# A convolution pair: the results' stores on GpSimd's queue, and the square of the Laplacian in the place of the smoothed sums

## The chip, the cores and the metric

The kernel runs on one core of one Trainium2 chip. The metric is device time in microseconds. The kernel before took 4897.4 us, the median of three runs (4884.03 to 4911.76 us).

The engines are TensorE (PE in the profile, its weight loads PEld), VectorE (DVE), ScalarE (ACT), GpSimd (POOL) and SyncE (SP), which here only issues transfers. Each takes its instructions in a fixed order.

## The reference

The input `x` has 4 images of 512 channels, 64 by 64 pixels, float32. Two layers follow each other.

Layer 0 is a linear attention: three 512 by 512 projections to queries, keys and values; a 5 by 5 depthwise and a grouped 1 by 1 convolution of these; an attention over 128 heads of 8 channels; a projection with batch normalisation; and `x` added. Call its result y. Layer 1, cut to what matters:

```python
sobel_h = dwconv(x, K_SX)
sobel_v = dwconv(x, K_SY)
sobel = jnp.sqrt(sobel_h ** 2 + sobel_v ** 2 + 1e-08)
lap = jnp.abs(dwconv(x, K_LAP))
diag = jnp.maximum(jnp.abs(dwconv(x, K_D1)), jnp.abs(dwconv(x, K_D2)))
grad = jnp.sqrt(sobel ** 2 + lap ** 2 + 1e-08)
E = jnp.stack([sobel, lap, diag, grad])
y = jnp.einsum('kbchw,koc->kbohw', E, w_branch) + b_branch[:, None, :, None, None]
# batch normalisation and Gelu; a gate per channel from the image's mean
z = jnp.einsum('bchw,oc->bohw', ef, w_fuse) + b_fuse[None, :, None, None]
mu = z.mean(axis=1, keepdims=True)
var = ((z - mu) ** 2).mean(axis=1, keepdims=True)
zn = (z - mu) / jnp.sqrt(var + LN_EPS)
out = jax.nn.gelu(zn * ln_gamma[None, :, None, None] + ln_beta[None, :, None, None], approximate=False)
return out + x
```

## The kernel before, in words

Channels lie on the 128 partitions, four chunks of 128 to an image. Layer 0 goes image by image in four groups of heads (`Group`): projections (L268, L290), the convolution as small matmuls (L402), correlations (L457), divisions; GpSimd issues the copies of the projected strips (L283), SP the loads of `x` and of `near` (L442).

Layer 1 of an image has three stages, each a Python generator. `project_out` makes y and writes it to DRAM. `edge_branches` reads windows of y and makes the four edge maps (`edges`), which TensorE takes to the branches (L738); `store` writes them out. `fuse_out` loads them (L892), multiplies by the fusion weights (`fuse`, L850), normalises, adds y and stores the result (`norm`).

For images 0 to 2 these stages are spread by shares of time (`advance`, SHARE_ and WAIT_ constants) between the steps of the next image's layer 0. For the last image nothing follows: its edge maps are made in windows of 8 rows instead of 4 and interleaved with its own projection and then with the third image's fusion, and its own fusion ends the kernel. TensorE's order is that of the program (`manual_schedule`). The order on the other engines comes from a scheduler that works from the dependences between tiles, so an edit of one tile can reorder them.

`edges` works on a window of two chunks. `dv` (one buffer) holds `down` and `smooth`, the differences and the sums of rows (L707 to L709). `maps` (three buffers) takes the diagonal and one Sobel term (L714), the Laplacian `lap` (L716 to L718) and the other Sobel term (L728, L729). ScalarE squares the Laplacian into `lap2` (L720), takes absolute values (L724) and squares the Sobel terms (L730). VectorE adds these (L731) and makes `grad` from `lap2` and the sum (L733), and ScalarE takes the roots (L734). With one `dv`, the next window's L707 has to wait for the last use of this one's.

`fuse` evicts each product twice, as a square (L852) and as `z` (L855 or L857, eight or six `z` buffers). `norm` takes the variance matmul (L866), its root (L868) and reciprocal (L869), multiplies (L877), takes Gelu (L878), and adds y from `yr`, which has two buffers (L874, L881). Then SP stores `z` (L882). A piece is 512 pixels of all four chunks; the very last 512 are two pieces of 256. There are 132 stores in all. One image's `fuse` of a piece is followed by the `norm` of the piece before.

All pools of layer 1 are stacks in SBUF, so a tile that is gone moves those behind it. TensorE's results go to PSUM, where the tag `ps` has four banks.

Of the kernel before, what the change touches and what calls it, by code (L numbers as in the profile page):

```python
# [8 lines left out]
F32 = mybir.dt.float32  # L9
# [6 lines left out]
P = 128  # L16
# [73 lines left out]
def conv_seq_kernel(  # L90
    ctx: ExitStack, tc, x, wqkv, dpk, wtab, proj, projc, pwk, bn0, consts, vec, watt1, batt1, watt2, wbr, wfuse, out
):
    nc = tc.nc
# [18 lines left out]
    def ps_tile(name):  # L112
        return psum.tile([P, 512], F32, tag="ps", name=name)
# [8 lines left out]
    def rows(ap, width=W):  # L122
        return ap.rearrange("p (r c) -> p r c", c=width)
# [99 lines left out]
    first = ExitStack()  # L223
# [449 lines left out]
    def edge_branches(b, efs, pool_sb, side):  # L673

        y = ys[b % 2]
        with ExitStack() as stack:
            pool = stack.enter_context(tc.tile_pool(name=f"E{b}", bufs=2, side=side, reuse_waits="tile"))
# [8 lines left out]
            run = WB * tall - 2  # L686
            yield 0.0

            def edges(u, pair):

                win = pool.tile([P, 2, (tall + 2) * WB], F32, name="win", tag="win")
                nc.sync.dma_start(
                    out=win,
                    in_=y[2 * pair : 2 * pair + 2].rearrange("c p r w -> p c (r w)")[
                        :, :, tall * u * WB : (tall * u + tall + 2) * WB
                    ],
                )
                above, mid, below = (win[:, :, n * WB : (n + tall) * WB] for n in range(3))
                maps = pool.tile([P, 4, 2, tall * WB], F32, name="maps", tag="maps", bufs=3)
                flat = maps.rearrange("p k c x -> p (k c x)")  # L700
                lap, sobel, grad = (maps[:, n, :, 0:run] for n in (0, 2, 3))


                dv = pool.tile([P, 2, 2, tall * WB], F32, name="dv", tag="dv", bufs=1)
                down, smooth = dv[:, 0], dv[:, 1]
                dvs = dv.rearrange("p k c x -> p (k c x)")
                nc.vector.tensor_sub(down, below, above)  # L707
                nc.vector.tensor_add(smooth, below, above)
                nc.vector.scalar_tensor_tensor(smooth, mid, 2.0, smooth, ALU.mult, ALU.add)  # L709

                half = 2 * tall * WB
                nc.vector.tensor_sub(flat[:, half : 3 * half - 2], dvs[:, 2 : 2 * half], dvs[:, 0 : 2 * half - 2])  # L714

                nc.vector.tensor_add(lap, mid[:, :, 0:run], mid[:, :, 2 : run + 2])  # L716
                nc.vector.scalar_tensor_tensor(lap, mid[:, :, 1 : run + 1], -6.0, lap, ALU.mult, ALU.add)
                nc.vector.tensor_add(lap, lap, smooth[:, :, 1 : run + 1])  # L718
                lap2 = pool.tile([P, 2, run], F32, name="lap2", tag="lap2", bufs=1)
                nc.scalar.activation(lap2, lap, AF.Square)  # L720
                first, second = (
                    maps[:, n : n + 2].rearrange("p k c x -> p (k c) x")[:, :, 0:run] for n in (0, 2)
                )
                nc.scalar.activation(first, first, AF.Abs)  # L724


                sv = flat[:, 3 * half : 4 * half - 2]
                nc.vector.tensor_add(sv, dvs[:, 0 : half - 2], dvs[:, 2:half])  # L728
                nc.vector.scalar_tensor_tensor(sv, dvs[:, 1 : half - 1], 2.0, sv, ALU.mult, ALU.add)  # L729
                nc.scalar.activation(second, second, AF.Square)  # L730
                nc.vector.tensor_add(sobel, sobel, grad)  # L731

                nc.vector.scalar_tensor_tensor(grad, lap2, SOBEL_EPS, sobel, ALU.add, ALU.add)  # L733
                nc.scalar.activation(second, second, AF.Sqrt, bias=sobel_eps)  # L734
                return maps
# [25 lines left out]
            if side == "left":  # L761

                banks = None
                for n in range(2 * steps + 1):
                    made = edges(n // 2, n % 2) if n < 2 * steps else None
                    yield 1.0
                    if n:
                        u, pair = divmod(n - 1, 2)
                        if pair == 0:
                            banks = quad_tiles("br")  # L770
                        for k in (1, 2, 0, 3):
                            for c in (2 * pair, 2 * pair + 1):
                                product(banks[k], k, c, held)
                        if pair:
                            for ks in ((1, 2), (0, 3)):
                                store(u, ks, [banks[k] for k in ks])
                    held = made
                yield 0.0
                return

            held = []
            for u in range(steps + 1):
                first = [edges(u, 0)] if u < steps else []
                yield share if u else share + WAIT_E
                if held:
                    branches(u - 1, (1, 2), held)
                    yield share
                    branches(u - 1, (0, 3), held)
                    yield share
                if first:  # L790
                    held = first + [edges(u, 1)]
                    yield share if u else share + WAIT_E

    def fuse_out(b, efs, pool_sb, side):

        y = ys[b % 2]
        with ExitStack() as stack:
            pool = stack.enter_context(tc.tile_pool(name=f"F{b}", bufs=2, side=side, reuse_waits="tile"))
# [63 lines left out]
            def norm(piece, zs, total):  # L862
                j, first, end = piece
                n, high = end - first, (end - first) // W
                ps = ps_tile("var")[:, :n]
                nc.tensor.matmul(ps, lhsT=ones, rhs=total, start=True, stop=True)  # L866
                rstd = pool.tile([P, 512], F32, name="rstd", tag="rstd", bufs=1)[:, :n]
                nc.scalar.activation(rstd, ps, AF.Sqrt, bias=ln_eps, scale=1.0 / C)  # L868
                nc.vector.reciprocal(rstd, rstd)  # L869
                at = 8 * j + first // W + 1  # L870
                for c in range(NCH):
                    z = zs[c]
                    yr = pool.tile([P, 8 * WB], F32, name="yr", tag="yr")[:, : high * WB]
                    nc.sync.dma_start(  # L874
                        out=yr, in_=y[c].rearrange("p r w -> p (r w)")[:, at * WB : (at + high) * WB]
                    )
                    nc.vector.tensor_mul(z, z, rstd)  # L877
                    nc.scalar.activation(  # L878
                        z, z, AF.Gelu, bias=vec_sb[:, V_LNB, c : c + 1], scale=vec_sb[:, V_LNG, c : c + 1]
                    )  # L880
                    nc.gpsimd.tensor_add(rows(z), rows(z), rows(yr, WB)[:, :, 1 : W + 1])  # L881
                    nc.sync.dma_start(out=out[b, c, :, 512 * j + first : 512 * j + end], in_=z)  # L882

            held = None
            for piece in pieces + [None]:
                if piece:
                    j, first, end = piece
                    n = end - first
                    ef = []
                    for k in range(4):  # L890
                        t = pool.tile([P, 512], F32, name="ef", tag="ef", bufs=8)[:, :n]
                        nc.sync.dma_start(out=t, in_=efs[j][:, k, first:end])  # L892
                        ef.append(t)
                    zs = []
                    total = pool.tile([P, 512], F32, name="total", tag="total")[:, :n]
                    fuse(0, ef, zs, total, n)
                    yield share
                    fuse(1, ef, zs, total, n)
                    yield share
                else:  # L900
                    yield 6.0
                if piece and late:
                    fuse(2, ef, zs, total, n)
                    yield share
                if held:
                    norm(*held)
                    yield share
                if piece:
                    for c in range(3 if late else 2, NCH):
                        fuse(c, ef, zs, total, n)  # L910
                        yield share
                    held = piece, zs, total
# [210 lines left out]
```

## Time and profile before

| what | value |
|---|---|
| median of three runs | 4897.4 us |
| the profiled execution, its own time | 4899.17 us |
| its span, first to last instruction | 4897.4 us |
| busy, TensorE / VectorE / ScalarE / GpSimd | 4649.1 / 2100.3 / 1592.8 / 1112.1 us |
| results' stores on SP (L882) | 132, 337 to 433 ns each to issue |
| strips' and maps' stores on GpSimd (L283, L751) | 1024 and 112, median 533 and 744 ns each to issue |
| L733, once a window | 112, of them 16 in the last image |

A line of a group gives the line of the kernel, engine, operation, the tile written and those read, the count and the durations. A line of waits gives who waited for whom, the total in us, how often, and the longest. A line of a timeline gives start and length in us, then engine, line and operation. A wait is put down to the engine whose event came last, and idle time of an engine that isn't on the path costs nothing.

### The profile page before, as it was taken

How to read it: one execution, taken by the hardware profiler on the slowest of the kernel's cores; microseconds unless marked ns; L12 is line 12 of the kernel's file. 1: busy time of each engine (PE TensorE's matmuls, PEld its weight loads, DVE VectorE, ACT ScalarE, POOL GpSimd, SP SyncE). 2: the span in 40 equal slices, each digit the busy share in tenths (PEclk: the TensorE clock that was granted, in tenths of full speed). 3: DMA queues.
4: the chain of work that ended last, by engine and by line, in shares of the span. 5: the costliest groups of instructions: out<-in, count | busy, mean ns of one | idle time of the engine just before them, and what ended most of it. 6: DMA issues, size and time to landing. Idle time of an engine off the chain costs nothing. (4 is left out here: it accounts for less than half of the span.)

```text
span 4897.4 us, 107513 instructions
## 1 busy us (share of the span) xinstructions
PE 4649.1 (95%) x46140; PEld 2691.9 (55%) x46140; DVE 2100.3 (43%) x2788; ACT 1592.8 (33%) x2723; POOL 1112.1 (23%) x1535
## 2 busy tenths in 40 slices
PE   9999999999999999899899999999999999899987
PEld 5666655455666565454466666455446565444433
DVE  1222222114655625311356553441125656437966
ACT  2111111002544524300245453430014545214765
POOL 3222212111221214311122121441112211011443
PEclk9999999999999999999999999999999999999998
DMA  6444456565656666676466666567556555554445
GB/s 204 136 126 136 141 182 199 163 165 157 206 174 202 188 207 187 214 188 171 142 200 195 190 195 203 175 210 211 153 172 186 183 174 176 164 160 148 158 146 171
DMA packets 469228, 864.12 MB, mean 176 GB/s; under 512 B 193000, under 2 KB 225800, under 8 KB 450320
## 3 DMA queue, kind: packets, MB, share of 16 engines
q1 hardware_dynamic: 415760, 721.90, 48.8%
q0 software_dynamic: 52992, 135.35, 9.0%
q8 instruction: 363, 5.95, 0.5%
q14 instruction: 113, 0.93, 0.1%
HBM read 575.93 MB, written 213.98 MB: 161 GB/s over the span
## 5 line engine op out<-in xcount | busy, mean ns | idle before, releaser
L268 PE MATMUL proj<-xt,w_sb 128*128 128x512 f32 x2048 | 937.6, 601 | 17.3 <-ACT rq L279 6.9
L661 PE MATMUL yps<-hd,fold_sb 128*128 128x512 f32 x2048 | 905.4, 599 | 18.4 <-DMA hd<-heads 14.9
L283 POOL DMA_DIRECT2D inp<-strip x1024 | 546.4, 536 | 1285.2 <-ACT strip L274 1253.5
L402 PE MATMUL cv<-inp,mat 32*32 32x512 f32 (+1 forms) x20480 | 734.5, 597 | 62.8 <-issue 50.2
L661 PEld LDWEIGHTS yps<-hd,fold_sb 128*128 128x128 f32 x2048 | 386.7, 191 | 508.1 <-issue 464.3
L268 PEld LDWEIGHTS proj<-xt,w_sb 128*128 128x128 f32 x2048 | 377.0, 191 | 475.2 <-issue 447.4
L402 PEld LDWEIGHTS cv<-inp,mat 32*32 32x32 f32 x20480 | 439.6, 103 | 325.7 <-issue 172.1
L850 PE MATMUL zps<-ef,wf_sb 128*128 128x512 f32 (+1 forms) x1056 | 467.2, 595 | 29.2 <-ACT z L855 17.2
L290 PEld LDWEIGHTS val<-w_sb,xt 128*128 128x128 f32 x4096 | 469.8, 192 | 34.4 <-issue 20.2
L290 PE MATMUL val<-w_sb,xt 128*128 128x128 f32 x4096 | 484.4, 277 | 0.5 <-DVE z L857 0.5
L274 ACT COPY strip<-proj 128x512 f32<-128x512 f32 x256 | 149.0, 582 | 989.9 <-PE proj L268 950.8
L738 PE MATMUL br<-maps,wbr_sb 128*128 128x256 f32 (+1 forms) x1792 | 468.3, 414 | 0.3 <-ACT ef_o L746 0.3
L666 DVE SCALAR_TENSOR_TENSOR yt<-yps,shift,xr 128x512 f32<-128x512 f32 x128 | 95.9, 749 | 837.2 <-PE yps L661 816.3
L738 PEld LDWEIGHTS br<-maps,wbr_sb 128*128 128x128 f32 x1792 | 337.6, 191 | 139.0 <-issue 98.4
L457 PE MATMUL corr<-near,ckt 128*32 128x160 f32 x8192 | 332.2, 315 | 32.9 <-DMA near<-near 21.5
L850 PEld LDWEIGHTS zps<-ef,wf_sb 128*128 128x128 f32 x1056 | 202.9, 195 | 273.4 <-issue 228.6
L670 POOL DMA_DIRECT2D y<-yt x128 | 114.7, 896 | 967.0 <-DVE yt L666 798.3
L714 DVE TENSOR_TENSOR maps<-dv 128x1054 f32<-128x1054 f32 (+1 forms) x112 | 159.7, 1425 | 391.0 <-PE br L738 390.9
L457 PEld LDWEIGHTS corr<-near,ckt 128*32 128x32 f32 x8192 | 256.2, 111 | 128.1 <-issue 66.5
L751 POOL DMA_DIRECT2D ef<-ef_o x112 | 81.8, 730 | 659.9 <-ACT ef_o L746 636.6
L318 ACT ACTIVATE kt<-tr 128x512 f32<-128x512 f32 x128 | 75.9, 593 | 471.3 <-PE tr L316 471.3
L881 POOL TENSOR_TENSOR z<-z,yr 128x512 f32<-128x512 f32 (+1 forms) x132 | 176.4, 1353 | 227.1 <-ACT z L878 125.1
(131 smaller groups left out, 4378.2 us busy)
## 6 DMA issues: line engine op xcount, KB each, us to landing
xt<-in_x SPq DMA_DIRECT2D x316, 512.0 KB
near<-near SPq DMA_DIRECT2D x512, 264.0 KB
inp<-strip POOLq DMA_DIRECT2D x1024, 64.0 KB, 4.2
win<-y SPq DMA_DIRECT2D x96, 396.0 KB
near<-vt SPq DMA_DIRECT2D x512, 66.0 KB
y<-yt POOLq DMA_DIRECT2D x128, 264.0 KB, 6.5
heads<-q SPq DMA_DIRECT2D x128, 256.0 KB
cheads<-cq SPq DMA_DIRECT2D x128, 256.0 KB
```

The lines of the kernel that those rows point to most:

```text
L268: nc.tensor.matmul(ps, lhsT=self.w[t][:, c, :], rhs=xs[self.b, j][c], start=(c == 0), stop=(c == NCH - 1))
L274: nc.scalar.copy(s, ps)
L283: nc.gpsimd.dma_start(out=inps[t][r::4, n, b : b + 8, :], in_=rows(s)[32 * n : 32 * n + 32, :, :])
L290: nc.tensor.matmul(ps[:, ts(c, P)], lhsT=xs[self.b, j][n][:, ts(c, P)], rhs=self.w[VALUE][:, n, :], start=(n == 0), stop=(n == NCH - 1),)
L402: nc.tensor.matmul(rows(banks[i])[32 * j : 32 * j + 32, :, c0:c1], lhsT=self.mat[t][q, j, (dx + 2) * 8 + 4 * b : (dx + 2) * 8 + 4 * b + 4, :],
L457: nc.tensor.matmul(self.banks[jj][32 * i : 32 * i + 32, 160 * b : 160 * b + 160], lhsT=self.held["c", i][:, at : at + 32], rhs=v[:, 4 * n ...
L661: nc.tensor.matmul(ps, lhsT=fold_sb[g // NG][:, g % NG, ts(c, P)], rhs=hd[g], start=(g == 0), stop=(g == 2 * NG - 1),)
L670: nc.gpsimd.dma_start(out=y[c, :, at : at + 29 : 4, :], in_=yt)
L714: nc.vector.tensor_sub(flat[:, half : 3 * half - 2], dvs[:, 2 : 2 * half], dvs[:, 0 : 2 * half - 2])
L738: nc.tensor.matmul(rows(ps), lhsT=wbr_sb[:, k, c, :], rhs=rows(maps[:, slot[k], c % 2, :], WB)[:, :, 0:W], start=(c == 0), stop=(c == NCH ...
L850: nc.tensor.matmul(ps, lhsT=wf_sb[:, k, ts(c, P)], rhs=ef[k], start=(k == 0), stop=(k == 3))
L881: nc.gpsimd.tensor_add(rows(z), rows(z), rows(yr, WB)[:, :, 1 : W + 1])
```

## The change

Two edits. The square of the Laplacian has no tile of its own any longer: it is written into `dv`, over the first part of `smooth`, whose last reader (L718) comes before it. And the result's store is issued by GpSimd instead of SP.

```diff
@@ in edges @@
                 nc.vector.tensor_add(lap, lap, smooth[:, :, 1 : run + 1])
-                lap2 = pool.tile([P, 2, run], F32, name="lap2", tag="lap2", bufs=1)
+                lap2 = smooth[:, :, 0:run]
                 nc.scalar.activation(lap2, lap, AF.Square)
@@ in norm @@
                     nc.gpsimd.tensor_add(rows(z), rows(z), rows(yr, WB)[:, :, 1 : W + 1])
-                    nc.sync.dma_start(out=out[b, c, :, 512 * j + first : 512 * j + end], in_=z)
+                    nc.gpsimd.dma_start(out=out[b, c, :, 512 * j + first : 512 * j + end], in_=z)
```

## The prediction

> **What bounds the kernel now.** I read the page's busy line first, then the table of stretches for the two stages that the change touches alone, then the waits.
>
> ```profile
> PE 4649.1 (95%) x46140; PEld 2691.9 (55%) x46140; DVE 2100.3 (43%) x2788; ACT 1592.8 (33%) x2723; POOL 1112.1 (23%) x1535
> ```
>
> and from the table of stretches
>
> ```profile
> 4532.00:4742.00 210.00, 187.93 (x434) 81.50 (x432) 182.73 (x123) 157.34 (x191) 98.81 (x58) 0.95 0.46 148
> 4742.00:4898.00 156.00, 124.63 (x306) 60.29 (x306) 100.24 (x116) 83.47 (x110) 50.95 (x44) 0.89 0.55 171
> ```
>
> TensorE is busy 4649 of 4897.4 us, and its instruction order is the same in both built programs. Only its 248 us of idle time can shrink, and the change can only add to it. In these two rows the columns are stretch, length, then PE, PEld, DVE, ACT and POOL busy. The first row is the last image's edge maps with the third image's fusion between them: DVE is nearly full (183 of 210) and PE idles 22 us. The second is the last fusion and the drain, PE idle 31 us.
>
> The waits, over the whole span (total, times, longest):
>
> ```profile
> PE zps L850 <- ACT z L855: 17.2, 5, 6.3
> ...
> ACT maps L734 <- DVE maps L733: 82.5, 47, 5.3
> ...
> DVE z L857 <- DMA out<-z: 75.1, 40, 5.8
> POOL z L881 <- DMA yr<-y: 70.1, 25, 6.3
> ```
>
> and SP's own queue:
>
> ```profile
> SPq L882 <- POOL z L881: 343.3, 121, 15.0
> ```
>
> ScalarE stands at its square root until DVE has written `grad` (L733). TensorE waits for evictions of the fusion that stand behind it on ScalarE, all 17.2 us of them in the first of the two stretches. The stores do hold SP for 343 us, and a new `z` waits for an old store 40 times.
>
> One such place, on DVE's timeline; ScalarE's L734 idles 7.00 us ahead of 4683.86, until L733 is done, and TensorE is idle 6.00 us before 4688.41:
>
> ```profile
> 4675.97 1.24 DVE L717 SCALAR_TENSOR_TENSOR maps<-win,maps 128x1052 f32<-128x1052 f32 x1
> 4677.14 1.24 DVE L731 TENSOR_TENSOR maps<-maps 128x1052 f32<-128x1052 f32 x1
> 4678.30 3.34 DVE L714 TENSOR_TENSOR maps<-dv 128x2110 f32<-128x2110 f32 x1
> 4681.56 2.22 DVE L733 SCALAR_TENSOR_TENSOR maps<-lap,maps 128x1052 f32<-128x1052 f32 x1
> ```
>
> The price of a transfer issued by GpSimd is read from the edge maps' own stores (L751; issue time, then landing, each min/median/max):
>
> ```profile
> L751 POOL DMA_DIRECT2D ef<-ef_o x112: 562/744/767, 1207.7 to 4729.8; - x112
> ...
> DMA to landing us min/median/max: 2.5/4.2/8.6
> ```
>
> **What the Trainium skill says.** "DMA: Bandwidth & Descriptors", section "Latency and other measured facts": first byte about 1 us from GpSimd's software path, about 0.6 us from SP's hardware path. The trace gives the order of it: 4.2 us median above, against about 3.5 us for one of SP's stores (issued 4869.86; DVE's eviction that waited for a store goes on at 4873.34; that it is this store is my reading). "SBUF — State Buffer", section "Who interferes with whom": a VectorE operation with two SBUF inputs contends with a GpSimd instruction that reads SBUF, and descriptor generation is shut out only by VectorE's two-port modes. The trace agrees: GpSimd's add takes 1.18 us alone and some 2.3 beside DVE, and DVE's 1.24 us operations then take 2.2 to 2.3; but L670's issue takes 885/887/935 ns however busy DVE is, and DVE's 1.24 us at 4458.96 is not longer beside the 0.91 us issue at 4459.34. So the new issues cost GpSimd their own length and DVE nothing.
>
> **The stores, part by part.** 132 stores leave SP (0.34 us each) and come to GpSimd, each right behind its own add. At L751's 0.74 us that is 132 x 0.74 = 98 us more on GpSimd, 1112 to 1210 us, or 25%. In the first stretch it is 32 x 0.74 = 24 on top of 99 of 210 us. Behind a store on GpSimd stand the next add, the sum of squares (L860) and, in the middle images, the copies of strips (L283); four adds and four issues are 4 x (1.2 + 0.74) = 7.8 us of a 14.6 us piece, so GpSimd has room. Behind those wait the variance matmul (3.6 us of TensorE waits on it before) and a convolution that starts several projections later.
>
> SP is freed less than 343 us suggests. The built order leaves the loads of `yr` (two buffers) where they were, and `yr` for the third and fourth chunk needs the first and second add just as the stores did. The longest such case is one load of `near`: TensorE waited 10.24 us for it until 2043.66; on SP three parts go out from 2028.48, then two stores (2033.80), two `yr`, and the last part at 2036.42. Afterwards the same two `yr` still stand ahead of that part, the second now behind add, store, add: 2032.6 + 1.2 + 0.74 + 1.2 = 2035.7, plus 0.4 = 2036.1. I put this at 0 us, range -5 to 0.
>
> A `z` comes free later: 4.2 - 3.5 = 0.7 us of landing, and 0.7 for the second chunk, whose add stands behind a store; the third and fourth gain it back, as their `yr` is asked for one add earlier. Where the pieces are 512 wide this hides behind TensorE's four PSUM banks: from 4742 to 4829 six pieces ran with a single idle of 1.05 us, although DVE was waiting for stores. In the drain with its pieces of 256 the cover is gone: TensorE waited 2.34 and 2.96 us for L857 there. Two hand-overs at 1.4 make +3 us; with about 0.2 x 5 for the wide ones, +4 in all. The bounds are 0 and, with no cover at all, 9 pieces x 3 us = +27. The very end: last adds at 4892.99, stores landed at 4897.4; `yr` 1.2 earlier, issue 0.4 and landing 0.7 later: 0.
>
> **The squares in `smooth`, part by part.** The same instructions run on the same sizes, so no busy time changes. What changes is how long the one `dv` is held: until L733 instead of L718 and L729. In the built order L707 of the next window stood ahead of L733 in 88 of 108 places; now in none. L716 (40 before, 52 now) and L717 (10, 36) take some of the room. Other operations between L731 and L733 fall from 125 to 79.
>
> Gain: `grad` comes 1 to 3 operations sooner, 1.2 us each in the wide windows, and ScalarE's 127 us of idling at L734 (82.5 above and 44.4 at its table load) shrinks. In the first stretch that idling was 21.8 us; I take back 4 of TensorE's 17.2 us there.
>
> Loss: between L729 and L731 ScalarE must square 2104 columns (1.96 us), and L733 needs the other square too (1.06 us). L707 to L709, 3 x 1.17 = 3.5 us, used to cover that. The cover now is L714 and L718 (2.3 + 1.2), which the order puts after L729 in 7 of 15 wide windows, and L716 and L717. Where it is missing, or ScalarE has Gelu ahead, DVE stands still about 1 to 2 us: 16 wide windows, 8 uncovered, 1 us each = 8; DVE ends its last window 37 us before the stretch does, and GpSimd's adds use DVE's pauses without stretching it, so I count +3. Bounds 0 and 16 x 2 = 32.
>
> In the 96 narrow windows a pause is half as long (1.08 us square), and DVE has stood 391 us waiting for TensorE to release maps, so no map gets late. What remains is that reciprocals, products and evictions of the attention shift by about 1 us either way. TensorE's waits on these (its rows that name `rq`, `co`, `rec`, `weighed`, `q`, `cq` and `ckt`, summed) are some 85 us; I take 0, with ±10.
>
> Sum: 0 + 4 + 0 - 4 + 3 + 0 = +3 us on the profiled 4897.4 us span. That execution took 4899.2 us by its own time and the median of the runs is 4897.4, so I say 4900 us.
>
> **Rivals.**
>
> Faster, by ScalarE unblocked (0.24): if every stall behind L734 goes as at 4683, TensorE's waits for evictions and DVE (17 in the first stretch, 85 in the attention) fall by about a third, 34 us, less 4 for stores: 4868. For it: 127 us of idling at one line. Against it: most of that is not on TensorE's path.
>
> Slower, by DVE pausing (0.18): in the wide windows L731 and L733 wait for ScalarE, which is 75% busy there (157 of 210). At 2 us for each of 16 windows +32, thus 4930. It decides from about 1.5 us a window, when 37 us of spare DVE time and the gaps in PE's order no longer take it up. For it: DVE is at 183 of 210. Against it: 52 places hold L716 in the gap.
>
> Slower, by late `z` (0.10): if landings in the last fusion are nearer the 8.6 us maximum than 4.2, each of nine pieces finds its `z` 4.4 us later; a third of that hidden, the 3 us of the bound, 27 us, thus 4925. It decides once the banks' cover is used up, of which 1.05 us of idle in six pieces says that little is left. Against it: at most half of the DMA time is busy there.
>
> That the sharing of memory changes nothing but addresses, and the stores likewise, is inside my forecast (0.48).
>
> **How the numbers follow.** The forecast's own range is 4885 to 4915. What a measurement of this kernel can tell from no change is about 0.5%, 24 us (the three runs spread over 28). Faster gets 0.23 (its rival but for the part that stays within), same 0.50, slower 0.27 (both slow rivals less a little). For 8 in 10 the range must reach well into both sides, from 4870 to 4934.
>
> **What would show it.** Right: about 132 GpSimd issues at L882 of 0.6 to 0.8 us landing after 3 to 5; SP waiting at L874 for L881 about as long as at L882 before; L707 always after L733; DVE waits on L730 or L720 growing from 13.7 us to some tens; PE busy the same within 10 us. Wrong: SP's waits really gone and `near` no longer waited for; DVE idle in 4532 to 4742 rising by over 20 us; waits of L857 for stores doubling and TensorE idle between the wide pieces; or GpSimd's issues lengthening beside DVE.

## The result, and the profile after

The changed kernel takes 4913.4 us (median of 20 runs, 4900.14 to 4928.18), the kernel before 4897.41 us in the same session (20 runs). The ratio is 1.0032 with a 95% interval of 1.0020 to 1.0043: some 16 us more, by the interval 10 to 21, and within the 0.5% that was called no change. The profiled execution took 4905.17 us by its own time.

From the page of the kernel after, the busy line:

```profile
PE 4658.4 (95%) x46140; PEld 2700.9 (55%) x46140; DVE 2108.4 (43%) x2788; ACT 1590.0 (32%) x2721; POOL 1163.1 (24%) x1667
```

and its table of stretches for the two stages (stretch, length, then PE, PEld, DVE, ACT and POOL busy, TensorE's granted clock as a share of full speed, share of DMA time, GB/s):

```profile
4525.00:4736.00 211.00, 188.65 (x433) 81.96 (x431) 180.78 (x123) 157.40 (x191) 95.03 (x82) 0.95 0.47 149
4736.00:4903.30 167.30, 129.09 (x306) 61.91 (x306) 99.61 (x117) 83.29 (x110) 72.93 (x88) 0.87 0.53 159
```

The edge maps of the last image take what they took (211.0 us against 210.0, TensorE idle 22 us in both). The last fusion has grown from 156.0 to 167.3 us. Counted from the last attention product (L826) to the end, which I use as the length of the last fusion from here on, it went from 159.6 to 171.5: +11.9 us.

The waits of the kernel after, over the whole span (total, times, longest):

```profile
DVE z L857 <- DMA out<-z: 136.8, 57, 6.8
...
ACT maps L734 <- DVE maps L733: 31.2, 23, 3.7
ACT L734 <- DVE maps L733: 30.9, 17, 7.7
...
DVE maps L731 <- ACT maps L730: 29.4, 40, 2.1
...
PE zps L850 <- DVE z L857: 20.9, 7, 5.8
...
PE zps L850 <- ACT z L855: 16.3, 3, 11.2
```

VectorE now waits 137 us instead of 75 for stores to give back `z`, and TensorE waits 20.9 us instead of 6.4 for VectorE's L857. ScalarE's idling at its root (L734) halved, from 127 to 62 us. SP's own queue:

```profile
SPq L874 <- POOL z L881: 309.4, 111, 18.4
```

SP stands for the same adds, now ahead of the loads of `yr`, for 309 us where it stood 343 ahead of the stores. The stores themselves, as the page of their line gives them (nanoseconds min/median/max to issue, then issue to landing):

```profile
L882 POOL DMA_DIRECT2D out<-z x132: 542/557/582, 1833.3 to 4899.1; - x132
...
DMA to landing us min/median/max: 2.0/4.0/8.8
```

And one 512-wide piece of the last fusion, first on VectorE, then on GpSimd, and where TensorE stands meanwhile:

```profile
4816.09 3.34 DVE L869 RECIPROCAL rstd<-rstd 128x512 f32<-128x512 f32 x1
...
4820.00 2.49 DVE L877 TENSOR_TENSOR z<-z,rstd 128x512 f32<-128x512 f32 x4
...
4828.40 0.75 DVE L857 TENSOR_SCALAR z<-zps,fbias 128x512 f32<-128x512 f32 x1 [5.31 <-DMA out<-z]
...
4830.47 0.75 DVE L857 TENSOR_SCALAR z<-zps,fbias 128x512 f32<-128x512 f32 x1 [0.72 <-DMA out<-z]
...
4833.55 0.75 DVE L857 TENSOR_SCALAR z<-zps,fbias 128x512 f32<-128x512 f32 x1 [1.74 <-DMA out<-z]
```

```profile
4822.95 1.19 POOL L881 TENSOR_TENSOR z<-z,yr 128x512 f32<-128x512 f32 x1 [7.50 <-ACT z L878]
4824.43 0.56 POOL L882 DMA_DIRECT2D out<-z  x1 [0.30 <-POOL z L881]
...
4826.50 0.56 POOL L882 DMA_DIRECT2D out<-z  x1 [0.30 <-POOL z L881]
```

```profile
4829.20 15.70 PE L850 MATMUL zps<-ef,wf_sb 128*128 128x512 f32 x32 [3.04 <-DVE z L857]
```

GpSimd waits 0.30 us after its own add before the store, which takes 0.56 us to issue. The store of 4824.43 lets VectorE go on at 4828.40, 3.97 us later. Counted from the piece's first L877, the `z` of the first chunk is back after 8.40 us, that of the second after 10.47 (store issued 4826.50, `z` taken 4830.47) and that of the third after 13.55 (issued 4828.90, taken 4833.55). Now a piece of the kernel before in which VectorE waits for the stores too, SP's queue first:

```profile
4839.16 1.92 SPq L882 DMA_DIRECT2D out<-z  x2
```

```profile
4835.01 2.49 DVE L877 TENSOR_TENSOR z<-z,rstd 128x512 f32<-128x512 f32 x4
...
4841.30 0.75 DVE L857 TENSOR_SCALAR z<-zps,fbias 128x512 f32<-128x512 f32 x1 [1.61 <-DMA out<-z]
...
4843.04 0.75 DVE L857 TENSOR_SCALAR z<-zps,fbias 128x512 f32<-128x512 f32 x1 [0.39 <-DMA out<-z]
```

The eight `z` buffers go round in order, so these two evictions take the buffers of the first and the second chunk: back after 6.29 and 8.03 us, 2.14 and 2.30 us after the stores were issued (the second at 4840.74, an issue of 0.34 us before the end of its row). So `z` is late by 2.1 and 2.4 us; the third chunk's, which was back after 12.87 (taken 4847.88), is less than 1 us late.

The landings bear this out. Each store raises a semaphore sixteen times, and the last of these comes 1.7/2.2/6.6 us (min/median/max of 132) after the start of the issue from SP, and after 2.0/4.0/8.8 us from GpSimd. In both kernels every wait for a store in the last fusion ends 0.10 to 0.13 us after the landing of the store eight evictions before.

In the kernel after, VectorE idles 5.31 us in front of the first of the new evictions, and TensorE 3.04 us before 4829.20. That wait is new, and it returns from piece to piece.

### The profile page after: what moved, and what is told of

Same layout as the page of the kernel before. It is cut to its first block, busy times and chain, and to the rows that moved or that the text cites. A ratio compares the mean times of both kernels' runs of the same rounds, so it can differ in the third digit from the quotient of the medians.

```text
span 4903.3 us, 107585 instructions
## 1 busy us (share of the span) xinstructions
PE 4658.4 (95%) x46140; PEld 2700.9 (55%) x46140; DVE 2108.4 (43%) x2788; ACT 1590.0 (32%) x2721; POOL 1163.1 (24%) x1667
## 5 line engine op out<-in xcount | busy, mean ns | idle before, releaser
L268 PE MATMUL proj<-xt,w_sb 128*128 128x512 f32 x2048 | 938.3, 601 | 17.3 <-ACT rq L279 6.9
L402 PE MATMUL cv<-inp,mat 32*32 32x512 f32 (+1 forms) x20480 | 736.1, 599 | 56.7 <-issue 43.7
L402 PEld LDWEIGHTS cv<-inp,mat 32*32 32x32 f32 x20480 | 444.5, 103 | 317.1 <-issue 165.5
L850 PE MATMUL zps<-ef,wf_sb 128*128 128x512 f32 (+1 forms) x1056 | 474.3, 603 | 42.9 <-DVE z L857 20.9
L457 PE MATMUL corr<-near,ckt 128*32 128x160 f32 x8192 | 333.8, 316 | 33.4 <-DMA near<-near 22.7
L714 DVE TENSOR_TENSOR maps<-dv 128x1054 f32<-128x1054 f32 (+1 forms) x112 | 159.7, 1426 | 369.1 <-PE br L738 369.1
L751 POOL DMA_DIRECT2D ef<-ef_o x112 | 81.7, 729 | 660.4 <-ACT ef_o L746 623.7
L746 ACT ACTIVATE ef_o<-br,shift,scale 128x256 f32<-128x256 f32 (+1 forms) x224 | 131.4, 590 | 265.9 <-PE br L738 265.5
```

The source lines that it names most:

```text
L268: nc.tensor.matmul(ps, lhsT=self.w[t][:, c, :], rhs=xs[self.b, j][c], start=(c == 0), stop=(c == NCH - 1))
L402: nc.tensor.matmul(rows(banks[i])[32 * j : 32 * j + 32, :, c0:c1], lhsT=self.mat[t][q, j, (dx + 2) * 8 + 4 * b : (dx + 2) * 8 + 4 * b + 4, :],
L457: nc.tensor.matmul(self.banks[jj][32 * i : 32 * i + 32, 160 * b : 160 * b + 160], lhsT=self.held["c", i][:, at : at + 32], rhs=v[:, 4 * n ...
L746: nc.scalar.activation(o[:, n, :], parts[n], AF.Gelu, bias=shift1[:, k : k + 1], scale=scale1[:, k : k + 1], accum_out=pool_sb[:, k, u : u ...
L850: nc.tensor.matmul(ps, lhsT=wf_sb[:, k, ts(c, P)], rhs=ef[k], start=(k == 0), stop=(k == 3))
```

## Experiments

Two theories. **Late z**: the time is lost where VectorE stands at L857 for a store that comes back later; the squares cost nothing or gain a little. **Squares**: `dv`, held until L733, costs the time. A third reading, **rescheduling**, is that the scheduler's order of the other engines shifts with any edit. It was in the expectations from the start and came to matter: the built order of VectorE and ScalarE in the last fusion is the same, instruction for instruction, in the kernel before and in those with the squares alone or the stores of images 0 to 2 alone, and another in every kernel with eight `z` buffers that stores the last image's results from GpSimd alone and leaves the order to the scheduler. No experiment leaves out any part of the computation. Times in us are the ratio's share of that session's median of the kernel before.

### The two edits apart

The stores alone (and for the last image alone: `nc.gpsimd if b == B - 1 else nc.sync`):

```diff
-                    nc.sync.dma_start(out=out[b, c, :, 512 * j + first : 512 * j + end], in_=z)
+                    nc.gpsimd.dma_start(out=out[b, c, :, 512 * j + first : 512 * j + end], in_=z)
```

> Only the stores are moved to GpSimd; the square keeps its own tile. Late z (the changed kernel's 12 us in the last fusion come from stores that give z back later): whole kernel +10 to +20 us against before, the last fusion from its first attention product to the end about 171 us against 159.6 before, VectorE waiting for stores at L857 about 137 us against 75. Squares (the single dv held to L733 costs it): within 5 us of before, last fusion about 160. Rescheduling alone (any edit moves the time by 10 us): no tie of the two numbers.

> Stores on GpSimd for the last image alone (36 of 132), square in its own tile. Late z: nearly all of the loss is here, +8 to +15 us, last fusion about 171 us, for in the other images TensorE has the next image's work between the pieces. If the loss were spread over all images by GpSimd's extra issues: under +5 us. Squares: 0.

The squares alone:

```diff
-                lap2 = pool.tile([P, 2, run], F32, name="lap2", tag="lap2", bufs=1)
+                lap2 = smooth[:, :, 0:run]
```

> Only the square goes where the smoothed sums were; stores stay on SP. Late z: same as before or up to 8 us faster, last fusion about 160 us, what lies ahead of the last fusion about 6 us shorter, as in the changed kernel's profile; VectorE's waits at L731 and L733 for ScalarE about 35 us against 13.7. Squares: +10 to +20 us against before, with TensorE idle in the last image's edge maps grown by more than 5 us over 22. Rescheduling alone: either sign.

The stores alone gave 1.0044 [1.0029, 1.0059], +21 us (1 above what was expected), last fusion 171.5 us. The last image's stores alone gave 1.0025 [1.0012, 1.0038], +12 us, last fusion 171.4; nearly all of the loss was expected there, and little more than half of it is. The squares alone gave 0.9985 [0.9975, 0.9995], -7 us, last fusion 159.7. The two edits pull in opposite directions, the stores carry the whole loss, and the "squares cost it" theory is out.

### Where the squares gain

```diff
-                lap2 = smooth[:, :, 0:run]
+                lap2 = smooth[:, :, 0:run] if tall == 4 else pool.tile([P, 2, run], F32, name="lap2", tag="lap2", bufs=1)
```

> Squares in the smoothed sums' place for the narrow windows of images 0 to 2 alone; the last image keeps the square's own tile; stores on SP. If the gain of the squares (0.9985) is ScalarE freed in the attention of the next image: TensorE's waits for ScalarE's co evictions (19.7 us before, 9.8 with all squares) fall to about 10 us here too, and most of the gain stays (0.9985 to 0.9995). If it comes from the last image's wide windows: those waits stay near 20 us, the whole at 1.000.

0.9987 [0.9974, 1.0000]: the narrow windows alone keep nearly the whole gain, as far as the interval can tell. TensorE's waits for `co` were 14.5 + 5.2 = 19.7 us before and are 8.0 + 4.5 = 12.5 here. TensorE's waits with all squares in place (same columns as above):

```profile
PE zps L850 <- ACT z L855: 12.8, 2, 10.2
...
PE cden L549 <- ACT co L421: 7.9, 4, 3.3
...
PE var L866 <- ACT z L855: 4.7, 1, 4.7
```

One place on ScalarE's timeline, before and then with the squares alone, in the second image's attention, where TensorE waits for L421 (6.07 us before, 2.84 with the squares):

```profile
1181.17 1.17 ACT L734 ACTIVATE maps<-maps,sobel_eps 128x1048 f32<-128x1048 f32 x1 [1.22 <-DVE s_sb L335]
1182.24 2.04 ACT L421 ACTIVATE co<-cv 128x512 f32<-128x512 f32 x4
```

```profile
1175.47 1.17 ACT L734 ACTIVATE maps<-maps,sobel_eps 128x1048 f32<-128x1048 f32 x1 [1.52 <-DVE maps L733]
1176.55 2.04 ACT L421 ACTIVATE co<-cv 128x512 f32<-128x512 f32 x4
```

The evictions of `co` (L421) stand behind L734, and L734 behind L733. (The first row names L335, which directly follows L733 on VectorE; L733 ended at 1181.08, L335 at 1181.17, and what L734 reads is what L733 writes.) From the first product of that convolution on TensorE (L402 at 1158.53 and at 1153.80) to the denominators (1182.87 and 1177.18) it took 24.34 us before and 23.38 with the squares, 23.37 in the changed kernel. So of the 3.2 us by which this wait is shorter some 1.0 is time won; where TensorE spends the rest was not traced. The same stretch ahead of two later waits for L421, of 2.84 and 4.93 us before, fell from 18.10 to 16.42 us and from 16.90 to 15.60. The three places together make 3.9 of the 7 us. The sign holds throughout: TensorE waits 17.1 to 19.7 us for `co` in the four kernels whose narrow windows have the square in its own tile, and 8.0 to 12.8 in the ten others. So the runs point to the narrow windows; that it is all ScalarE's idling at L734 is argued, not shown.

### The stores of the first three images

```diff
+                    (nc.sync if b == B - 1 else nc.gpsimd).dma_start(out=out[b, c, :, 512 * j + first : 512 * j + end], in_=z)
```

> Stores on GpSimd for images 0 to 2 (96 of 132), on SP for the last; square in its own tile. Late z in the drain is all: within 3 us of before, last fusion about 160 us. If GpSimd's 53 us of issues or later z cost time in the first three images too, as the gap between all stores (+21 us) and the last image's alone (+12 us) suggests: +6 to +12 us with the last fusion at 160 us.

1.0020 [1.0010, 1.0030], +10 us, last fusion 161.8. Of its +2.2 us, 2.1 lie behind the landing of the last store: from there to the end it takes 3.44 us against 1.35, in GpSimd's closing drain. So the last fusion is not all. Outside the last fusion TensorE's waits for VectorE's L857 are 2.1 us in the kernel before, 9.6 here, 10.0 with all stores moved and 9.6 in the changed kernel. Two of these waits on TensorE's timeline, and VectorE before them:

```profile
3155.01 0.66 PE L429 MATMUL ctr<-consts_sb,co 128*128 128x128 f32 x4 [1.57 <-DVE z L857]
3158.89 5.79 PE L850 MATMUL zps<-ef,wf_sb 128*128 128x512 f32 x8 [3.12 <-DVE z L857]
```

```profile
3151.57 0.75 DVE L857 TENSOR_SCALAR z<-zps,fbias 128x512 f32<-128x512 f32 x1 [6.50 <-DMA out<-z]
...
3158.09 0.75 DVE L857 TENSOR_SCALAR z<-zps,fbias 128x512 f32<-128x512 f32 x1 [3.13 <-DMA out<-z]
```

VectorE stands at one store after the other. What TensorE lacks here is not only room for the next `zps`: products of the next image's attention (`den`, `ctr`, `cden`) are held up by the same instruction.

### Late z, or a new order of VectorE

The last fusion's 36 evictions, 27 sums, 9 reciprocals and 36 multiplications on VectorE, and 81 activations on ScalarE, were tied to a given order by dependences that fix the order of issue on one engine and add no wait. GpSimd and SP were left free.

```diff
+            if b == B - 1:
+                in_order(tc, seen, "zztztztzztztrzmmmmtztztzrzmmmmttzztrzmmmmztztztzrzmmmmttzztrzmmmmztztztzrzmmmmtttzzrzmmmmztttzzrtmmmmzzrmmmm")
+                in_order(tc, seen, "sssssssqsggggsssqssggggssqsggggsssqssggggssqsggggsssqsssggggsqssggggssqsggggqgggg")
...
+def in_order(tc, seen, order):
+    left = {k: list(v) for k, v in seen.items()}
+    row = [left[k].pop(0) for k in order]
+    for later, sooner in zip(row[1:], row):
+        tc.add_manual_dep(
+            later.ins, sooner.ins.name,
+            mybir.DependencyInfo(mybir.DependencyClass.NoSync, mybir.DependencyReason.DATA), reason="order",
+        )
```

(`seen` collects the instructions by letter: z is L857, t L860, r L869, m L877; s L852, q L868, g L878.) The old order is that of the kernel before. In the new one wide pieces read "tztztzrzmmmm" one after the other, where the old one alternates "ttzztrzmmmmz" with "tztztzrzmmmm".

> The changed kernel, with VectorE's and ScalarE's instructions of the last fusion tied to the order they have in the kernel before; the stores stay on GpSimd. Late z: the order is not the cause, last fusion 168 to 172 us. If it was the scheduler's new order of VectorE (evictions of z and sums alternating, the reciprocal behind them) that cost the time: last fusion back to about 160 us and the whole about 12 us under the changed kernel.

> Squares in the smoothed sums' place, stores on SP, with VectorE's and ScalarE's instructions of the last fusion tied to the order that the changed kernel has. Late z: last fusion 158 to 162 us, whole as with the squares alone (0.9985 of before). New order as the cause: last fusion about 171 us and 8 to 12 us more than the squares alone.

The last fusion of the two, from the table of stretches (columns as above):

```profile
4706.10:4873.20 167.10, 127.79 (x311) 61.29 (x310) 105.03 (x123) 87.67 (x115) 75.10 (x89) 0.88 0.52 159
```

```profile
4705.80:4872.90 167.10, 129.63 (x311) 61.90 (x310) 102.64 (x123) 87.29 (x115) 50.61 (x45) 0.88 0.51 159
```

| last fusion, us | old order | new order |
|---|---|---|
| stores on SP | 159.6, 159.7, 160.4 | 167.1 |
| stores on GpSimd | 167.1 | 171.5, 171.5, 171.4 |

(Behind the last landing stand 1.3 us in each kernel of the upper row and 2.2 in those of the lower, but 4.0 in the one of 171.4, which stores the last image alone from GpSimd. So 0.8 us of a step from SP to GpSimd is this closing.)

Neither theory had this: each gives half. With the order held, GpSimd's stores cost 7.5 us in the old order and 4.4 in the new. With the stores held, the new order costs 7.5 on SP and 4.4 on GpSimd. As whole kernels they gave 1.0015 [1.0003, 1.0027] and 1.0002 [0.9992, 1.0011], +7 and +1 us. The terms agree within the intervals: -7 (squares) + 7.5 + 7.2 (waits for L857 outside the last fusion, 9.4 against 2.1 us) makes +8 us in the first, and -7 + 7.5 about 0 in the second, which stores from SP throughout.

### Which store decides

Three kernels hold the old order and differ in the last image's stores: the first two chunks of a piece on SP (`c < 2`), the last two on SP (`c > 1`), or all on GpSimd with four `yr` buffers.

```diff
+                    (nc.sync if b == B - 1 and c < 2 else nc.gpsimd).dma_start(out=out[b, c, ...], in_=z)
```

> The changed kernel in the old order of VectorE and ScalarE (last fusion 167.1 us), but in the last image SP stores the first two chunks of a piece, GpSimd the last two. If the 7.5 us over 159.6 come from the first two chunks' stores (0.84 and 1.77 us later than from SP, by the traces, counted from the piece's first multiplication to the next z): last fusion 158 to 161 us. If they come from the last two or from GpSimd's work in general: 164 us or more.

> The mirror image: GpSimd stores the first two chunks of a piece of the last image, SP the last two, in the old order. First two chunks as the cause: last fusion 165 to 169 us. Last two as the cause: 158 to 162 us.

```diff
+                    yr = pool.tile([P, 8 * WB], F32, name="yr", tag="yr", bufs=4 if b == B - 1 else 2)[:, : high * WB]
```

> The changed kernel in the old order with four yr buffers instead of two in the last image, so that no add waits for a load that waited for an earlier add. If the adds' waits for yr (0.3 to 1.7 us before the third and fourth) are part of what makes z late: last fusion 162 to 165 us. If add, store, add, store in one queue and the landing are all of it: 166 to 168 us.

Last fusion 172.2, 163.0 and 167.6 us (1.0020 [1.0007, 1.0034], 1.0013 [1.0000, 1.0027], 1.0023 [1.0010, 1.0036]). The first falls to its second branch, 164 us or more, but it is 5.1 us above the 167.1 that it started from, which neither branch had: giving the first two chunks back to SP made it worse. The second fell between its two branches. (The 0.84 and 1.77 us in the first expectation are misread: they set the first chunk's store on SP against the second chunk's eviction. It is 2.1 and 2.4 us, as above.) The reason for the first is on SP's, GpSimd's and VectorE's timelines of that kernel:

```profile
4809.65 1.92 SPq L882 DMA_DIRECT2D out<-z  x2
4811.61 7.14 SPq L874 DMA_DIRECT2D yr<-y  x4
```

```profile
4815.16 1.18 POOL L881 TENSOR_TENSOR z<-z,yr 128x512 f32<-128x512 f32 x1 [3.95 <-DMA yr<-y]
4816.64 0.56 POOL L882 DMA_DIRECT2D out<-z  x1 [0.30 <-POOL z L881]
```

```profile
4820.00 0.75 DVE L857 TENSOR_SCALAR z<-zps,fbias 128x512 f32<-128x512 f32 x1 [5.09 <-DMA out<-z]
4820.66 3.34 DVE L869 RECIPROCAL rstd<-rstd 128x512 f32<-128x512 f32 x1
```

The loads of `yr` stand behind both stores on SP, so GpSimd idles 3.95 us before the third add. In the wide pieces the third store is issued 9.9 to 12.3 us after the piece's first L877, against 7.6 to 10.0 with all stores on GpSimd. Here it gives `z` back at 4820.00, and only then comes the reciprocal that lets the next piece be normalised. As far as the timelines tell, this is the loop that sets the pace: reciprocal, multiplication, Gelu, add, store, return, eviction, and the next reciprocal behind that eviction on VectorE.

Moving the last two stores to SP instead takes 4.1 of the 7.5 us away, 1.2 of them behind the last landing; two more `yr` buffers take nothing (the third and fourth store are issued about 1.0 and 1.4 us sooner, the second 0.8 later, because the scheduler put two adds in a row). So no single chunk carries it, and which share each has is left open. Nor does a run separate the later issue from the longer way to landing; in the traces above the first chunk's 2.1 us are 0.28 of the one and 1.83 of the other.

### Two more buffers

```diff
-                z = pool.tile([P, 512], F32, name="z", tag="z", bufs=8 if late else 6)[:, :n]
+                z = pool.tile([P, 512], F32, name="z", tag="z", bufs=10 if b == B - 1 else 8 if late else 6)[:, :n]
```

Ten fit only because the squares' own tile is gone.

> The changed kernel with ten z buffers instead of eight in the last image, which fits because the square's own tile is gone. Late z: a store then has half a piece more time, more than the 3 to 5 us that VectorE waited for it; the last fusion falls from 171 to 158 to 164 us and the whole is 5 to 10 us faster than before. If GpSimd's adds and stores in a row set the pace instead (1.57 us a chunk in the drain), or the variance waits on it: the last fusion stays above 168 us and the whole stays at +10 to +16.

> Squares in the smoothed sums' place, stores on SP, ten z buffers in the last image. Late z: the last fusion gains less than the 18.6 us that ten buffers gave with GpSimd's stores, since z was less late; 150 to 155 us, and the whole 12 to 17 us under before (0.9965 to 0.9975), the best so far. If the buffers only cover what GpSimd's stores add: last fusion near 160 us and the whole as with the squares alone (0.9985).

With all of the change: 0.9986 [0.9972, 1.0000], -7 us as expected, last fusion 152.9 us, 5 below the range expected. With the stores on SP: 0.9973 [0.9959, 0.9987], last fusion 152.4. TensorE in the former (stores on GpSimd) now runs from piece to piece without a wait:

```profile
4774.03 13.90 PE L850 MATMUL zps<-ef,wf_sb 128*128 128x512 f32 x32
4787.77 1.02 PE L866 MATMUL var<-total,ones 128*128 128x512 f32 x2
4788.62 13.90 PE L850 MATMUL zps<-ef,wf_sb 128*128 128x512 f32 x32
```

A piece takes 14.59 us, TensorE's own time, against 17.3 to 18.1 in the changed kernel (reciprocals at 4798.75, 4816.09 and 4834.22). The stores still land in 3.9 us at the median; only nobody waits for them. Ten buffers also gave these kernels an order of their own, so the 18.6 us are buffers and order together. That the last fusion is 0.5 us apart with stores on GpSimd and on SP, in one and the same order of VectorE and ScalarE, shows that GpSimd's own work is no bound there. The squares with ten buffers and the stores on SP are the fastest version found, 13 us under the kernel before (6 to 20).

## Why the prediction was right, and where it was not

The time was called: 4900 with its own range of 4885 to 4915 and "same" as the likeliest; it is 4913.4, and the ratio is within 0.5%. The sum behind it was not: +3 was made of small terms, the measured +16 is a difference of two larger ones. So the number owes something to luck: the stores alone cost +21 us, which without the squares' -7 would have stood at 4918, outside the prediction's own range. And one of its own signs of being wrong came: VectorE's waits for stores at L857 went from 75 to 137 us, with TensorE idle between the wide pieces.

**SP freed: 0 us, -5 to 0.** Right. SP waits 309 us at L874 for the same adds, and TensorE's wait for `near` is 22.7 us against 21.5; the longest, 10.24 us before, is still 9.11.

**GpSimd +98 us, hidden.** Its length was too long: a store of 128x512 takes 0.557 us to issue, not L751's 0.74, so 73.8 us, and the adds became shorter (176.4 to 159.3 us in all), so GpSimd's busy time rose by 51. No cost by itself in the last fusion: with ten buffers the last fusion is the same from either queue.

**A later z: +4.** The mechanism was right, and its size at the source was too small: 0.7 and 1.4 us said for the first two chunks, 2.1 and 2.4 found. The 3.5 us taken for a store of SP set the first store of a row (issued 4869.86) against the eviction at 4873.34, which waited for the second, issued at 4871.00; that is 2.3 us, and SP's median is 2.2. So landing from GpSimd takes 1.8 us more, not 0.7. The other step that failed is "where the pieces are 512 wide this hides behind TensorE's four PSUM banks", +1 for the wide pieces. The banks cover one delay, but the delay comes back through the loop above in each piece, so that less and less is covered (a reading of the timelines): TensorE idles 3.30, 3.04 and 1.00 us between wide pieces where one wait of 1.05 was. In the last fusion the term is 4.4 to 7.5 us by the order of VectorE, 0.8 of it behind the last landing.

**A term that was not in the sum: the order of the last fusion.** The rescheduling of VectorE and ScalarE there is worth 4.4 to 7.5 us. The prediction read the built order around `dv` and took the rest as given.

**A second missing term: later z in images 0 to 2.** Behind a `z` on VectorE stood the next image's attention, and TensorE's waits for it went from 2.1 to 9.6 us. The step looked for GpSimd's followers (sums, strips) and not for VectorE's.

**The very end: 0.** Right: from the first of the last four adds to the end 9.84 us (4893.46 to 4903.3) against 9.39 (4888.01 to 4897.4). The 4897.4 is the end of the kernel, though, not the landing, which was at 4896.05.

**ScalarE unblocked: -4 of the 17.2 us at L855.** Right in kind, wrong in place. L734's idling halved, but the waits on L855 are 16.3 in the changed kernel, and 3.0 more moved to the variance product; with the squares alone 12.8 + 4.7. The gain is, as far as the runs tell, in the narrow windows, where 0 with ±10 was put: TensorE's waits for `co` fell from 19.7 to 8.0 us. The rival for this mechanism, 34 us, was five times too large.

**VectorE pausing: +3.** Waits at L731 and L733 for ScalarE rose from 13.7 to 35.1 us, as said, but the edge stretch is 1 us longer and the wide windows change nothing that can be measured (0.9985 with them, 0.9987 without).

Of the rivals, "slower by late z" named the right mechanism at 0.10 and the wrong cause for it: landings near 8.6 us were not needed; the median is 4.0, and SP's 2.2 made the difference.

By the measured terms: +11.9 (last fusion) + 7.5 (z outside it) - 7 (squares) = +12.4 us, against 16 (10 to 21).

## What to carry to other kernels

A store's queue is part of the loop that gives its buffer back. If an engine (VectorE here) already waits for stores, take the delay of the buffer once per turn of that loop as a bound (here 9 pieces x 2.4 = 22 us, of which 4.4 to 7.5 were found), ask what stands behind the waiting instruction, and price the cure too: two more buffers, with the order that came with them, were worth more than the whole change. When pairing a store with the wait that it ends, count the buffers round: a store taken for its neighbour made SP's way 1.2 us too long here. Where a scheduler orders the engines, compare its order in every stage that waits on the edited tile, and separate order from mechanism by holding the order fixed.

## What the runs showed of the hardware

- GpSimd needs 0.30 us from the end of its own add to the issue of the store of that result, then 0.557 us to issue it: 1.57 us a chunk of 128x256 with its 0.69 us add, in the drain.
- From issue to landing a store of results took 1.7/2.2/6.6 us (min/median/max) from SP in the kernel before and 2.0/4.0/8.8 us from GpSimd in the changed kernel, 132 stores each. The Trainium skill, "DMA: Bandwidth & Descriptors", "Latency and other measured facts", puts the first bytes of the two paths 0.4 us apart; the runs agree on which is slower, but the landings of these stores are 1.8 us apart at the median.
- The same 311 matmul records of the last fusion are busy 124.5 us where it lasts 152.4, and 130.8 us where it lasts 172.2, at granted clocks of 0.90 and 0.87; it is no strict rule, for where it lasts 152.9 they take 125.3 us at 0.88. The Trainium skill, "TensorE: Matmul & The Clock Gate", "What's actually happening", says that activity releases the clock; that the pauses cause it here was not tested.
- From the landing of the last store to the end the kernel took 1.3 us where every store came from SP, 2.2 where every store came from GpSimd, and 3.4 or 4.0 where images 0 to 2 or the last image alone stored from GpSimd. The longer closings are GpSimd's drain.
- Up to the last landing, the last fusion's length repeats within 0.8 us (158.3 to 159.1) in the four kernels with the old order, eight buffers and the last image's stores on SP, while what lies ahead of it differs by 18 us between the profiled executions of two kernels that hardly differ there (4713.7 and 4731.8 us with and without two more buffers). A stage is the finer measure.
